# Seven block products for eight in the self-attention projections of a transformer block, with the context keys kept in device memory meanwhile

## The chip, the core and the metric

The kernel runs on one core of a Trainium2 chip. The core has a matrix engine (PE, with its weight loads shown as PEld), three engines for elementwise work (DVE, ACT and POOL) and an engine, SP, whose queue issues DMA transfers. Each engine takes its instructions in program order and waits on semaphores for the others. SBUF is the working memory of 128 partitions; PSUM, in eight banks of 512 fp32 values per partition, takes the matmul results. The metric is the device time of one execution in microseconds (us); a lower time is better.

## The reference

The reference is one transformer block in fp32 over x of shape (2, 1024, 256), with a context of shape (2, 154, 192): self-attention with 16 heads of 64, cross-attention to the context with as many heads, and a gated feed-forward.

```python
h = _layernorm(x, ln1_g, ln1_b)
x = _attention(h, h, sa_wq, sa_wk, sa_wv, sa_wo, sa_bo) + x
h = _layernorm(x, ln2_g, ln2_b)
x = _attention(h, cond_emb, ca_wq, ca_wk, ca_wv, ca_wo, ca_bo) + x
h = _layernorm(x, ln3_g, ln3_b)
p = h @ ff_w1 + ff_b1
a, gate = (p[..., :D_FF], p[..., D_FF:])
h = a * jax.nn.gelu(gate, approximate=False) @ ff_w2 + ff_b2
return h + x
```

Inside `_attention`, q = xq @ wq and k = xkv @ wk (256 or 192 channels by 1024 outputs), the scores are scaled by 1/8, go through a softmax and weigh v, and wo brings the result back to 256 channels. So the queries and keys of self-attention are two products of the same h with two weight matrices.

## The kernel before

The work on self-attention goes by units. A unit is one batch entry and one pair of heads, so there are 16 units, and a pair of heads has 128 columns of wq, of wk and of wv. The normalized tokens of a batch entry lie transposed in `hT`: 64 channels of one half of the tokens in the upper 64 partitions, the same 64 channels of the other half in the lower, and four blocks of channels side by side.

A unit has eight slots of 128 queries, p = 8 * unit + n with n from 0 to 7. The text below calls them slot 0 to slot 7. Every slot makes two groups of scores (`scores`, PE, L492; two PSUM banks for each group, two groups in all, so that a group can only be written once the exponents of the same group of the slot before have been read). DVE takes the maxima of each group (L501), ACT the exponents (L507: two instructions for each group, each with a read of its sum). The maxima and sums of the two halves of a row lie in different partitions, so four DMAs swap them (`exchange`, L517, on SP). POOL forms the differences (L525, L526), ACT their exponents (L532), POOL the denominators (L534, L536); this is done in the slot after. One slot later still, DVE takes the reciprocals (L604, between the two maxima), POOL scales the exponents with them (L612) and DVE transposes them (L639, two per slot). The transposed rows of four slots together are weighed with the values (`weigh`, PE, L546, one half in each of two slots).

The order of the instructions on each engine is the order in which the Python code emits them; no planner moves them. In the loop over p, `self_first` emits the scores and the maxima, `flush(stores)` emits copies out of PSUM that earlier pieces left, `then()` emits exponents, softmax steps, exchange and transposes, and after these comes a piece of PE work for the slot:

- slots 0, 3, 4 and 7: half of a `weigh`; the two copies of its result to SBUF (ACT, L678) come at the start of slots 1 and 5
- slot 1: the queries of the next unit (`self_queries`, L361, 64 matmul instructions of 512 columns)
- slot 2: the keys of the next unit (the same size)
- slot 5: the values of the next unit (L392), and one step of a norm running beside
- slot 6: two pieces of the output projection `py_sa` (L466), added to x by DVE (L473) one slot later each, and one step of a norm

The queries and keys go to two PSUM banks of the pool `mm`, and ACT copies them to SBUF at the start of the next slot (L376 with the scale, L384 with a regrouping of the keys); `weigh` and some other pieces use the two banks of the pool `po`. SP also issues the weights for the unit after next: wq in slot 2, wk in slot 3, wv in slot 7.

The context stage has 48 steps c, three for each unit (two of three tiles of tokens and one of two), with n = 0, 1, 2 within a unit. A step makes scores (L855), maxima (L860), exponents (L873) and, two steps later, transposes (L900). Eight DMAs regroup the transposed rows of a unit (`cross_regroup`, L917) into a buffer, `pairs`, that exists once; two steps later `cross_weigh` weighs the values with it (L938), with its first two results in the `po` banks and the other two in the `mm` banks, each copied by DVE (L955). For even units, `context_values` makes the values of two units (L813), ACT copies them (L823), and six DMAs complete them (L825, L830). The queries of the unit after next need a weight slice loaded by L133. Four output pieces of self-attention are left over at step 4; they run in steps 4 and 5. The context keys `kT` are computed during self-attention into an SBUF buffer of 320 columns for each of eight pairs. The gated feed-forward, which already uses seven products for eight, is last.

## Time and profile before

| | us |
|---|---|
| median of three runs | 1083.98 |
| lowest and highest of the three | 1083.78, 1085.25 |
| the profiled execution | 1085.11 |
| span of the profiled execution, first to last instruction | 1083.3 |
| PE busy in the span | 1067.4 |
| DVE busy | 889.9 |
| POOL busy | 765.0 |
| ACT busy | 646.9 |

The busy time of PE counts each matmul until its modelled end, and matmuls overlap, so a busy PE may still be issuing more slowly than it could; the distance between the starts of groups of matmuls says how fast it goes. A row of the timeline has its start in us from the start of the span, its length, engine, line, operation, the tiles written and read with their shapes, the number of merged instructions and, in brackets, how long the engine had been idle and what ended that. A row of the chain of work has start, length and what ran. A row of the waits has the waiting instruction, what it waited for, total us, times, and the longest. The clock granted to the matrix engine is 1.00 throughout.

### The profile page before, as it was taken

Reading aid. Unit: us, or ns where it says so; the run is one execution under the profiler, and the core shown is the slowest. Engines: PE = TensorE matmul, PEld = TensorE weight load, DVE = VectorE, ACT = ScalarE, POOL = GpSimd, SP = SyncE. Lnnn points to the kernel's source line nnn. Section 1 sums busy time; section 2 is a strip of 40 time slices with the busy share of each in tenths; the row PEclk is TensorE's granted clock in tenths of the full one; section 3 lists DMA queues with packets and bytes.
Section 4 is the critical chain, followed back from the end, with each engine's and each line's share of the span. In section 5 each row is a group of like instructions: output and inputs, shape, how many; then the busy total and the mean of one; then the engine's idle time right before and its main releaser. Section 6 shows DMA issues by size and latency. Waiting matters only on the chain.

```text
span 1083.3 us, 45246 instructions
## 1 busy us (share of the span) xinstructions
PE 1067.4 (99%) x18548; PEld 710.0 (66%) x18548; DVE 889.9 (82%) x1317; ACT 646.9 (60%) x2063; POOL 765.0 (71%) x1600
## 2 busy tenths in 40 slices
PE   8999999999999999999999999998999999999998
PEld 6556556566565565565675665575777767888998
DVE  5789999998998989999999989968877887655554
ACT  5666767677666666666776766666566554342221
POOL 2667777788777777777777777757665686388774
PEclk9999999999999999999999999999999999999999
DMA  3232111111111111211211201136855545000000
GB/s 94 64 90 62 44 43 44 37 38 43 33 43 24 43 43 33 48 42 29 48 41 26 53 14 37 24 96 139 202 134 138 126 115 131 17 6 15 20 11 30
DMA packets 105120, 62.84 MB, mean 58 GB/s; under 512 B 32266, under 2 KB 95506, under 8 KB 104914
## 3 DMA queue, kind: packets, MB, share of 16 engines
q1 hardware_dynamic: 103586, 59.29, 23.2%
q8 instruction: 146, 2.39, 0.9%
q10 hardware_dynamic: 1328, 0.66, 0.2%
q14 instruction: 60, 0.49, 0.1%
HBM read 30.01 MB, written 2.10 MB: 30 GB/s over the span
## 4 chain that ended last, share of the span: by engine, by line
PE 87%; DVE 3%; DMA 3%; POOL 3%; ACT 2%; SPq 1%; issue 1%; DVEq 0%; POOLq 0%; ACTq 0%
PE s L492 19%; PE po L546 19%; PE py_sa L466 5%; PE py_ca L466 5%; PE pv_sa L392 5%; PE pq_ca L361 4%; PE pq_sa L361 4%; PE pk_sa L361 4%; PE poc L938 4%; PE pb L1062 3%; PE pf L1186 3%; PE sc L855 3%; PE pa L1062 2%; PE pc L1062 2%; DMA st<-st 2%; PE pf L1225 1%
## 5 line engine op out<-in xcount | busy, mean ns | idle before, releaser
L612 POOL TENSOR_SCALAR p<-p,rd,ee 128x512 f32<-128x512 f32 x508 | 387.3, 773 | 99.1 <-DVE rd L604 97.3
L507 ACT ACTIVATE p<-s,st 128x512 f32<-128x512 f32 x512 | 345.8, 686 | 176.5 <-DVE st L501 170.5
L501 DVE TENSOR_REDUCE st<-s 128x2 f32<-128x1024 f32 x256 | 308.5, 1206 | 51.7 <-issue 20.1
L639 DVE STREAM_TRANSPOSE pT<-p 128x1024 f32<-128x1024 f32 x256 | 302.3, 1219 | 1.5 <-POOL p L612 1.5
L492 PE MATMUL s<-k_sa,q_sa 64*32 64x512 f32 x4096 | 255.4, 591 | 2.7 <-ACT p L507 2.1
L546 PE MATMUL po<-pT,v_sa 64*32 64x256 f32 x8192 | 238.6, 376 | 0.9 <-ACT p L873 0.9
L546 PEld LDWEIGHTS po<-pT,v_sa 64*32 64x32 f32 x8192 | 173.8, 106 | 74.9 <-issue 27.3
L492 PEld LDWEIGHTS s<-k_sa,q_sa 64*32 64x32 f32 x4096 | 81.6, 106 | 102.8 <-issue 53.5
L873 ACT ACTIVATE p<-sc,neg 128x154 f32<-128x154 f32 x256 | 96.5, 408 | 84.5 <-DVE rden L881 80.7
L884 POOL TENSOR_SCALAR p<-p,rden 128x154 f32<-128x154 f32 x256 | 97.3, 401 | 62.7 <-DVE rden L881 62.3
L507 ACT ACTIVATION_READ_ACCUMULATOR p<-s,st 128x1 f32 x512 | 103.2, 202 | 0.0
L525 POOL TENSOR_TENSOR dd<-st 128x8 f32<-128x8 f32 x128 | 25.8, 202 | 66.1 <-DMA st<-st 64.3
L392 PEld LDWEIGHTS pv_sa<-sa_wv,hT_ln 64*128 64x128 f32 x1024 | 58.6, 188 | 14.2 <-issue 10.9
L392 PE MATMUL pv_sa<-sa_wv,hT_ln 64*128 64x128 f32 x1024 | 61.8, 275 | 0.0
L860 DVE TENSOR_REDUCE neg<-sc 128x6 f32<-128x924 f32 (+1 forms) x48 | 48.0, 1001 | 14.5 <-PE sc L855 14.4
L466 PE MATMUL py_ca<-ca_wo,o_ca 128*128 128x256 f32 x256 | 59.9, 382 | 0.0
L466 PE MATMUL py_sa<-sa_wo,o_sa 128*128 128x256 f32 x256 | 59.5, 386 | 0.0
L466 PEld LDWEIGHTS py_sa<-sa_wo,o_sa 128*128 128x128 f32 x256 | 47.3, 190 | 17.8 <-issue 6.9
L361 PE MATMUL pq_ca<-hT_ln,ca_wq 64*128 64x512 f32 (+1 forms) x352 | 58.4, 590 | 0.5 <-DMA ca_wq<-in_L_xattn_ca_wq_dram 0.5
L873 ACT ACTIVATION_READ_ACCUMULATOR p<-sc,neg 128x1 f32 x256 | 57.2, 224 | 0.0
L361 PE MATMUL pq_sa<-hT_ln,sa_wq 64*32 64x512 f32 (+1 forms) x976 | 57.0, 586 | 0.0
L361 PE MATMUL pk_sa<-hT_ln,sa_wk 64*32 64x512 f32 x960 | 56.8, 590 | 0.0
(135 smaller groups left out, 1471.5 us busy)
## 6 DMA issues: line engine op xcount, KB each, us to landing
wf<-pT_ca SPq DMA_DIRECT2D x128, 128.0 KB, 2.4
v_sa<-v_sa SPq DMA_DIRECT2D x32, 256.0 KB, 3.8
st<-st SPq DMA_DIRECT2D x510, 1.0 KB, 1.9
sa_wq<-in_L_xattn_sa_wq_dram SPq DMA_DIRECT2D x32, 128.0 KB, 3.4
sa_wk<-in_L_xattn_sa_wk_dram SPq DMA_DIRECT2D x32, 128.0 KB, 3.6
sa_wv<-in_L_xattn_sa_wv_dram SPq DMA_DIRECT2D x32, 128.0 KB, 3.3
ca_wq<-in_L_xattn_ca_wq_dram SPq DMA_DIRECT2D x32, 128.0 KB, 4.4
wf<-in_L_xattn_ff_w_dram SPq DMA_DIRECT2D x12, 256.0 KB, 4.2
```

Of the source, the lines that this page charges most:

```text
L361: nc.tensor.matmul(pq[r][f:f + m, at:at + n], lhsT=wt[own, c, f:f + m], rhs=h[own, c, t0:t0 + n], start=(c == 0), stop=(c == NH - 1), tile ...
L392: nc.tensor.matmul(pv[r][:, i * P:(i + 1) * P], lhsT=h[own, c, i * P:(i + 1) * P], rhs=wt[own, c, :], start=(c == 0), stop=(c == NH - 1), ...
L466: nc.tensor.matmul(py[:, e * D:(e + 1) * D], lhsT=o[:, i, (t + e) * P:(t + e + 1) * P], rhs=wo[kind, b, g][:, i, :], start=(i == 0), stop= ...
L492: nc.tensor.matmul(sc[a4 * KB:(a4 + 1) * KB, j, :], lhsT=q[r, c:c + KB], rhs=k[r, h * HB:(h + 1) * HB], start=True, stop=True, tile_positi ...
L501: nc.vector.tensor_reduce(st[:, 0, 0, i, :], sc, AX.X, ALU.max, negate=True)
L507: nc.scalar.activation(pr[:, j, :], sc[:, j, :], AF.Exp, bias=st[:, 0, 0, i, j:j + 1], accum_out=st[:, 0, 1, i, j:j + 1],)
L546: nc.tensor.matmul(po[a2][d:d + KB, :QH // 2], lhsT=v[r, t, e, d:d + KB], rhs=pT[r, d // DH * NK + n, :], start=(t == 0 and e == 0), stop= ...
L612: nc.gpsimd.tensor_scalar(pr[:, j, :], pr[:, j, :], v["rd"][:, c:c + 1], v["ee"][:, 0, c:c + 1], op0=ALU.mult, op1=ALU.mult,)
L639: nc.vector.transpose(halves[h][:, :, c:c + KB], slot[p]["members"][i].rearrange("p j (n k) -> p (j n) k", k=KB))
L873: nc.scalar.activation(pr_[:, j, i, :T], sc[:, j, i * T:(i + 1) * T], AF.Exp, bias=neg[:, j, i:i + 1], accum_out=den[:, j, i:i + 1],)
L884: nc.gpsimd.tensor_scalar(pr_[:, j, i, :T], pr_[:, j, i, :T], rden[:, j, i:i + 1], 1.0, op0=ALU.mult, op1=ALU.mult,)
L1062: nc.tensor.matmul(into[:, :BT], lhsT=lhs, rhs=wh[pair][i], start=first, stop=True, skip_group_check=True)
```

## The change

Queries and keys of a unit are one product of a two by two block matrix (two halves of the tokens' blocks by two halves of the channels) with another (two halves of the channels by wq and wk). The new code forms this product with seven block products in place of eight. For each product, PE runs 16 matmuls of 256 columns (`product`, called 1 to 7). It applies to units 2 to 15; units 0 and 1 keep the old way.

- The sums of blocks are formed ahead by POOL: four of tokens for each batch entry (`held_tokens`, 128x512), and four of weights for each unit (`held_weights`, 128x256, mostly one each in slots 5, 6, 7 and 0). They lie in SBUF where `kT` was.
- In slot 1, behind the first two exponents, product 1 goes to one half of the two `mm` banks (`sums`), and ACT copies it to the queries. At the end of the slot products 2 and 5 go to the two halves of the `po` banks (`low`, `high`), product 6 adds to `sums`, and DVE joins `low` to the queries.
- At the start of slot 2, ACT copies `sums` and `high` out. Between the first and second exponents of slot 2, product 7 adds to `sums` and ACT copies the result to keys. At the end of the slot product 3 adds to `high`, product 4 to `sums`, DVE joins `high` to the queries, and POOL adds two halves of the keys (128x512). The last copy of keys, by ACT, follows in slot 3.
- The `mm` and `po` banks are no longer taken from pools, one tile a bank, but are two tiles of two banks each, of which `bank_of` hands out one bank and then the other.
- The context keys of pairs 0 to 5 are written to device memory when made, and come back by six DMAs in slots 4 to 7 of unit 14 and 0 and 1 of unit 15, when the sums are no longer needed; those of pairs 6 and 7 are made in place.
- In units 2 and 3, slot 6 takes two steps of the norm beside in place of one.
- In the context stage, the four left-over output pieces run one each in steps 4, 5, 7 and 10. In step 7 the values of unit 2 are made behind `cross_weigh` in place of before it. In units 4 and 5 the third step may also take a norm step that needs a bank.

```diff
--- before.py
+++ after.py
@@ -61,18 +61,24 @@
     small = ctx.enter_context(tc.tile_pool(name="small", bufs=4))
     pt_ = ctx.enter_context(tc.tile_pool(name="pt", bufs=2))
...
-    ps_m = ctx.enter_context(tc.tile_pool(name="ps_m", bufs=2, space=bass.MemoryType.PSUM))
-    ps_o = ctx.enter_context(tc.tile_pool(name="ps_o", bufs=2, space=bass.MemoryType.PSUM))
+    ps_2 = ctx.enter_context(tc.tile_pool(name="ps_2", bufs=1, space=bass.MemoryType.PSUM))
+    dram = ctx.enter_context(tc.tile_pool(name="dram", bufs=1, space=bass.MemoryType.DRAM))
     scored = ExitStack()
...
+    two = {what: ps_2.tile([P, 2, HB], F32, name=f"two_{what}") for what in ("mm", "po")}
+    turns = {"mm": 0, "po": 0}
+
+    def bank_of(what):
+
+        turns[what] ^= 1
+        return two[what][:, turns[what], :]
+
     def mm_tile(name):
-        return ps_m.tile([P, HB], F32, tag="mm", name=name)
+        return bank_of("mm")
 
     def sum_tile(name):
-
-        return ps_o.tile([P, HB], F32, tag="po", name=name)
-
+        return bank_of("po")
 
     xt = {
         (b, g): const.tile([P, GT, D], F32, tag=f"x{b}{g}", name=f"x{b}{g}")
...
     nc.gpsimd.memset(ctxT, 0.0)
-    kT = const.tile([P, NPAIR, B * TP], F32, tag="kT", name="kT")
+    keys = {"dram": dram.tile([P, NPAIR - 2, B * TP], F32, name="keys")}
+    held_sums = one.tile([P, NPAIR * B * TP], F32, tag="kT", name="sums")
+    last_sum = one.tile([P, 2, P], F32, tag="ws", name="last_sum")
+
+    def load_back(pr):
+
+        if pr == 0:
+            keys["sb"] = one.tile([P, NPAIR, B * TP], F32, tag="kT", name="kT")
+        nc.sync.dma_start(out=keys["sb"][:, pr, :], in_=keys["dram"][:, pr, :])
 
     def together(*pieces):
         dones = [piece() for piece in pieces]
...
+    HT = S // 4
+    tokens, seven = {}, {}
+
+    def held_tokens(b):
+
+        t = held_sums[:, :NH * S // 2].rearrange("p (k c t) -> p k c t", k=NH, c=NH // 2)
+        h = hT["sa", b]
+        h11, h12, h21, h22 = (
+            h[:, c:c + 2, j * HT:(j + 1) * HT] for c in (0, 2) for j in range(2))
+        tokens[b] = {
+            1: h11, 2: h21, 3: h22, 4: t[:, 2], 5: t[:, 0], 6: t[:, 1], 7: t[:, 3],
+        }
+        own = tokens[b]
+        sub = lambda x, y, z: lambda: nc.gpsimd.tensor_tensor(x, y, z, ALU.subtract)
+        return [
+            sub(own[5], h12, h11), sub(own[6], h22, own[5]), sub(own[4], h21, own[6]),
+            sub(own[7], h22, h12),
+        ]
+
+    def held_weights(pr):
+
+        t = held_sums[:, NH * S // 2:].rearrange("p (k c f) -> p k c f", k=2, c=2)
+        q, k = (wsl["sa", pr, what] for what in "qk")
+        seven[pr] = {
+            1: q[:, 0:2], 2: q[:, 2:4], 3: last_sum, 4: k[:, 2:4], 5: t[:, 0], 6: t[:, 1],
+            7: k[:, 0:2],
+        }
+        own = seven[pr]
+        tt = lambda x, y, z, op: lambda: nc.gpsimd.tensor_tensor(x, y, z, op)
+        return [
+            tt(own[5], own[7], own[4], ALU.add),
+            tt(own[6], own[5], own[1], ALU.subtract),
+            tt(own[7], own[1], own[7], ALU.subtract),
+            tt(own[3], own[2], own[6], ALU.subtract),
+        ]
+
+    def both_halves(x, j):
+        return x.rearrange("p (r u t) -> p u r t", r=2, u=2)[:, j]
+
+    def key_halves(x, j):
+        return x.rearrange("p (h r u n j) -> p u r n h j", h=2, r=2, u=2, j=KB)[:, j]
+
+    def projected(unit):
+
+        b, pr = unit
+        sums = two["mm"][:, :, :HT]
+        low, high = (two["po"][:, :, j * HT:(j + 1) * HT] for j in range(2))
+
+        def product(i, into, first):
+
+            wt, h = seven[pr][i], tokens[b][i]
+            for c in range(2):
+                for f in range(0, P, KB):
+                    for r in range(2):
+                        own = slice(r * HR, (r + 1) * HR)
+                        nc.tensor.matmul(
+                            into[f:f + KB, r, :], lhsT=wt[own, c, f:f + KB], rhs=h[own, c, :],
+                            start=(first and c == 0), stop=(c == 1),
+                            tile_position=(r * HR, f), skip_group_check=True,
+                        )
+
+        def queries(j):
+            return both_halves(qk["sa", b, pr][0], j)
+
+        def keys_of(j, src):
+
+            nc.scalar.copy(
+                key_halves(qk["sa", b, pr][1], j),
+                src.rearrange("p r (n h j) -> p r n h j", h=2, j=KB))
+
+        def start():
+            self_unit(b, pr)
+            product(1, sums, True)
+            nc.scalar.activation(queries(0), sums, AF.Copy, scale=scale)
+
+        def join(src, j):
+            nc.vector.scalar_tensor_tensor(
+                queries(j), src, scale, queries(j), op0=ALU.mult, op1=ALU.add)
+
+        def first():
+            product(2, low, True)
+            product(5, high, True)
+            product(6, sums, False)
+            join(low, 0)
+
+            def store():
+                nc.scalar.activation(queries(1), sums, AF.Copy, scale=scale)
+                keys_of(0, high)
+
+            stores.append(store)
+
+        def middle():
+            product(7, sums, False)
+            keys_of(1, sums)
+
+        def last():
+            product(3, high, False)
+            product(4, sums, False)
+            join(high, 1)
+            k = qk["sa", b, pr][1].rearrange("p (h r u t) -> p u h r t", h=2, r=2, u=2)
+            nc.gpsimd.tensor_tensor(k[:, 1], k[:, 1], k[:, 0], ALU.add)
+            kept.append(lambda: keys_of(0, sums))
+
+        return start, first, middle, last
...
-    def exponents(u, sc, st, i):
+    def exponents(u, sc, st, i, between=None):
 
         pr = pp_.tile([P, 2, HB], F32, tag="P", name=f"p_{u}")
         for j in range(2):
+            if j and between:
+                between()
             nc.scalar.activation(
                 pr[:, j, :], sc[:, j, :], AF.Exp, bias=st[:, 0, 0, i, j:j + 1],
                 accum_out=st[:, 0, 1, i, j:j + 1],
@@ -694,8 +815,10 @@
             reciprocals(p - 2)
         maxima(sc[1], st, 1)
 
-        def then():
-            members = [exponents(f"{p}_0", sc[0], st, 0)]
+        def then(between=None, behind=None):
+            members = [exponents(f"{p}_0", sc[0], st, 0, between)]
+            if behind:
+                behind()
             softmax_steps(p)
...
-            work.extend(nxt)
+            work.extend(nxt[2:] if ui else nxt)
...
-        return lambda: nc.scalar.copy(kT[:, pr, :], pk[:, :B * TP])
+
+        def store():
+            own = keys["sb" if "sb" in keys else "stage"][:, pr, :]
+            nc.scalar.copy(own, pk[:, :B * TP])
+            if "sb" not in keys:
+                nc.sync.dma_start(out=keys["dram"][:, pr, :], in_=own)
+
+        return store
...
-        q, k = qk["ca", b, pr], kT[:, pr, b * TP:b * TP + T]
+        q, k = qk["ca", b, pr], keys["sb"][:, pr, b * TP:b * TP + T]
...
-                other = kT.rearrange("p a b -> p (a b)")[:, :NF * BT].rearrange(
+                other = keys["sb"].rearrange("p a b -> p (a b)")[:, :NF * BT].rearrange(
                     "p (f t) -> p f t", f=NF)
...
+        keys["stage"] = p2.tile([P, NPAIR - 2, B * TP], F32, tag="hT", name="keys_stage")
         stats, deviation, normalize, turn = norm_pieces("sa", 0, True)
         spare["bank"] = sum_tile
...
+        parts_of, sums_due, due = {}, {}, {}
+        for i, slot_of in enumerate((3, 4, 5, 6)):
+            sums_due.setdefault(slot_of, []).append((held_tokens, 0, i))
+        for i, (u, n) in enumerate(((NPAIR - 2, 3), (NPAIR - 2, 4), (NPAIR - 2, 7), (NPAIR - 1, 0))):
+            sums_due.setdefault(u * 2 * SH + n, []).append((held_tokens, 1, i))
+        for ui in range(2, NU):
+            at = ((ui - 2) * 2 * SH + n for n in ((7, 7, 8, 8) if ui == 2 else (5, 6, 7, 8)))
+            if ui == NPAIR:
+                at = ((ui - 2) * 2 * SH + n for n in (5, 6, 8, 9))
+            for i, p in enumerate(at):
+                sums_due.setdefault(p, []).append((held_weights, units[ui][1], i))
         for p in range(SA):
             if p % (2 * SH) == 0:
                 self_beside(p // (2 * SH))
@@ -1308,19 +1450,35 @@
                 held.clear()
             then = self_first(p)
             flush(stores)
-            then()
+            ui, n = divmod(p, 2 * SH)
+            steps = None
+            if 0 < ui < NU - 1 and n in (1, 2):
+                steps = parts_of[ui + 1] = parts_of.get(ui + 1) or projected(units[ui + 1])
+            if steps and n == 1:
+                then(behind=steps[0])
+            elif steps:
+                then(between=steps[2])
+            else:
+                then()
             if adds:
                 adds.pop(0)()
             flush(kept)
-            ui, n = divmod(p, 2 * SH)
             if later and (p < 4 or n in (2, 4, 6) and p < SA - 2):
                 later.pop(0)()
             if p in ahead:
                 ahead[p]()
+            for fn, of, i in sums_due.get(p, ()):
+                if i == 0:
+                    due[fn] = fn(of)
+                due[fn][i]()
             load_ahead(p)
-            if p < 2 * SH - 1 or p % SH in (1, 2):
-
-                run_work(2 if p < SA - SH else 1, n > SH or p < SH, sum_tile)
+            if SA - SH - 8 <= p < SA - SH - 2:
+                load_back(p - SA + SH + 8)
+            if steps:
+                steps[1 if n == 1 else 3]()
+            elif p < 2 * SH - 1 or p % SH in (1, 2):
+
+                run_work(2 if p < SA - SH else 1, (1 + (ui in (2, 3) and n == SH + 2)) * (n > SH or p < SH), sum_tile)
                 if p == LAG:
                     load_weights("sa", units[1][1], "v")
                 if p == 3 * SH + 2:
@@ -1398,16 +1556,19 @@
                 run_work(0, 1, sum_tile if outs else None)
                 flush(stores)
                 run_work(0, 0, n_sum=1)
-                if ui % 2 == 0:
+                if ui % 2 == 0 and ui > 2:
                     run(lambda: context_values(*units[ui]))
-                run_work(1, 0)
+                if ui > HP + 1:
+                    run_work(1, 0)
                 flush(adds)
                 flush(stores)
                 cross_weigh(c)
+                if ui == 2:
+                    run(lambda: context_values(*units[ui]))
             elif n == 2:
-                run_work(0, 1, sum_tile if ui == HP + 1 else None)
+                run_work(0, 1, sum_tile if HP < ui < 3 * HP else None)
                 if c == SH + 1:
-                    run_work(2, 0)
+                    run_work(1, 0)
                 elif ui > HP and ui % HP == 1:
                     load_out("ca", *divmod(ui // HP - 1, NQ))
             cross_regroup(c)
```

## The prediction

> **What bounds the kernel now.** I read the page first, for the busy shares and the chain that ended last.
>
> ```profile
> span 1083.3 us, 45246 instructions
> PE 1067.4 (99%) x18548; PEld 710.0 (66%) x18548; DVE 889.9 (82%) x1317; ACT 646.9 (60%) x2063; POOL 765.0 (71%) x1600
> PE 87%; DVE 3%; DMA 3%; POOL 3%; ACT 2%; SPq 1%; issue 1%; DVEq 0%; POOLq 0%; ACTq 0%
> sa_wq<-in_L_xattn_sa_wq_dram SPq DMA_DIRECT2D x32, 128.0 KB, 3.4
> ```
>
> PE carries 87% of the chain. By this view, PE work taken away is time taken away. Whether that holds in the slots where the change works is seen in the timeline of one unit: slot 1 starts at 408.39, slot 2 at 413.54, slot 3 at 418.69.
>
> ```profile
> 405.14 3.45 PE po L546 x128
> ...
> 410.89 2.80 ACT p L507 x8
> ```
>
> ```profile
> 408.39 1.92 PE L492 MATMUL s<-k_sa,q_sa 64*32 64x512 f32 x32
> 409.07 0.65 DVE L473 TENSOR_TENSOR x<-py_sa,x 128x512 f32<-128x512 f32 x1
> 409.65 1.21 DVE L501 TENSOR_REDUCE st<-s 128x2 f32<-128x1024 f32 x1
> 410.11 3.64 PE L361 MATMUL pq_sa<-hT_ln,sa_wq 64*32 64x512 f32 x64
> 412.01 2.36 DVE L639 STREAM_TRANSPOSE pT<-p 128x1024 f32<-128x1024 f32 x2
> 413.54 1.92 PE L492 MATMUL s<-k_sa,q_sa 64*32 64x512 f32 x32
> 413.84 1.09 ACT L376 ACTIVATE q_sa<-pq_sa 128x512 f32<-128x512 f32 x2
> 414.77 1.22 DVE L501 TENSOR_REDUCE st<-s 128x2 f32<-128x1024 f32 x1 [0.40 <-ACT q_sa L376]
> 416.03 0.69 ACT L507 ACTIVATE p<-s,st 128x512 f32<-128x512 f32 x1 [1.10 <-DVE st L501]
> 417.11 2.36 DVE L639 STREAM_TRANSPOSE pT<-p 128x1024 f32<-128x1024 f32 x2
> 418.60 0.21 ACT L507 ACTIVATION_READ_ACCUMULATOR p<-s,st 128x1 f32 x1
> 418.69 1.92 PE L492 MATMUL s<-k_sa,q_sa 64*32 64x512 f32 x32
> ```
>
> The first fence is the chain of work (start, length, what), the second the timeline. A slot lasts 5.15: scores 1.72 (410.11 - 408.39), then a projection of 3.43 (413.54 - 410.11). PE issues without a gap. But DVE works from 414.77 to 419.47 in slot 2, 4.70 of 5.15, and ACT reads its last sum at 418.81, 5.27 after the slot's start. The slot's own chain (scores, maxima, exponents, next scores) is thus nearly as long as PE's work. An earlier slot that happens to have little PE work shows what that chain allows:
>
> ```profile
> 94.65 1.95 PE L492 MATMUL s<-k_sa,q_sa 64*32 64x512 f32 x32
> 99.73 0.21 ACT L507 ACTIVATION_READ_ACCUMULATOR p<-s,st 128x1 f32 x1
> 100.00 1.09 PE L492 MATMUL s<-k_sa,q_sa 64*32 64x512 f32 x16 [0.25 <-ACT p L507]
> ```
>
> The second group of the next slot starts 5.35 after this slot's start, 0.06 after ACT's last read, and PE waited for ACT. In a normal slot that group starts at 5.15 + 0.86 = 6.01 (0.86 is half of the scores' 1.72). So the reserve of a slot is 0.66, and no saving beyond it can arrive.
>
> The waits between 62 and 691 us say how often the reserve is touched:
>
> ```profile
> PE s L492 <- ACT p L507: 1.0, 4, 0.3
> ...
> DVE rd L604 <- POOL den L536: 10.5, 21, 1.5
> ```
>
> DVE waits 10.5 us for denominators, PE only 1.0 for the exponents behind them: the reserve now swallows nearly all of it.
>
> **The change part by part.** *Products.* `weigh` has 128 instructions of 256 columns in 3.45, 27 ns each. A product is 32 instructions, 0.86; seven are 6.04 where queries and keys take 2 x 3.43 = 6.86. PE saves 0.82 for each of 14 units, 11.5 us. Slot 1 becomes 1.72 + 4 x 0.86 = 5.17 and slot 2 1.72 + 3 x 0.86 = 4.31: the whole saving lies in slot 2.
>
> *What arrives of it.* In slot 2 a copy of keys now stands on ACT between the first two exponents; half of the 1.09 at 413.84 is 0.545. The chain of slot 2 becomes 5.35 + 0.545 = 5.90, against 6.01 now. PE will stand still for 5.90 - 4.31 - 0.86 = 0.73 before the second scores of slot 3 (or partly earlier, at product 4, which needs that copy too), and 0.11 of the 0.82 arrives: 14 x 0.11 = -1.5 us.
>
> *Product 6 in slot 1* overwrites what ACT copies to the queries behind two exponents. These start 2.50 after the slot's start (410.89) and four take 2.7 of the row's 2.80, so two end at 3.84, the copy at 4.39, and 0.05 later PE may go; it arrives at 1.72 + 3 x 0.86 = 4.31. That is 0.13 in each unit, bounds 0 and 0.3: +1.8 us.
>
> *Joins on DVE*, two in each unit. Their form (128x512, PSUM and SBUF in) has no row; the bounds are these, and I take 0.65, the row of equal width.
>
> ```profile
> L473 DVE TENSOR_TENSOR x<-py_sa,x 128x512 f32<-128x512 f32 x24 | 15.6, 652 | 0.0
> L1101 DVE SCALAR_TENSOR_TENSOR own<-pb,cols,own 128x256 f32<-128x256 f32 x14 | 6.8, 484 | 12.2 <-PE pb L1062 12.1
> L1153 POOL TENSOR_TENSOR wx<-wf,wx 128x512 f32<-128x512 f32 x2 | 2.5, 1274 | 0.0
> L319 POOL TENSOR_TENSOR x<-x,sa_bo 128x256 f32<-128x256 f32 x16 | 11.7, 731 | 0.0
> ```
>
> The lower bound is 0.48, the upper twice that. The add at 409.07 holds DVE 0.58 (to 409.65). DVE's slot of 4.70 becomes 5.28, longer than slot 1 (5.17) and than slot 2. Slot 1's transposes end at 414.37, its join at about 414.95, and slot 2's maxima could start at 414.77 + 0.13: no reserve is left. Any lateness of the denominators in slots 1 to 3 now reaches PE. That is 42 of about 120 slots, so 10.5 x 42 / 120 = 3.7 us exposed; some of it overlaps with waits counted above. I take +2.5 us, bounds 0 and 7.4 (twice 3.7, since exponents of slots 1 and 2 also end 0.55 later, and the exchange behind them).
>
> *POOL* gets four sums of 0.73 in slots 5, 6, 7 and 0, an addition of 1.27 in slot 2, and eight token sums of 1.27 in all. The sums of 0.73 stand where the bias additions of equal length stand today without PE waiting. The addition of 1.27 stands ahead of the scaling in slot 3, and with the later exponents of slot 2 it delays the denominators that slot 4 needs. +1.0 us, bounds 0 and 3.
>
> *Context keys.* Six writes and six reads of 160 KB (128 partitions x 320 x 4 B) join SP's queue, one in a slot, behind that slot's exchange; the nearest row is wq with 128 KB and 3.4 us. They are needed only later; they can delay a swap of maxima. +0.3 us, bounds 0 and 1.5. The new home of the PSUM banks, the FF's use of the returned tile, and the doubled norm steps (the same instructions, earlier) I set at nothing: PE has its full list of work in those slots.
>
> *Context stage.* Around steps 7 to 12, PE waits:
>
> ```profile
> 733.64 1.01 PE L855 MATMUL sc<-kT,q_ca 64*128 64x154 f32 x12
> 735.64 1.09 PE L938 MATMUL poc<-wf,v_ca 64*64 64x256 f32 x16
> 738.95 0.87 PE L938 MATMUL poc<-wf,v_ca 64*64 64x256 f32 x10 [1.36 <-ACT v_ca L823]
> 746.38 0.65 PE L938 MATMUL poc<-wf,v_ca 64*64 64x256 f32 x4 [0.19 <-DMA wf<-pT_ca]
> 750.32 0.86 PE L938 MATMUL poc<-wf,v_ca 64*64 64x256 f32 x10 [0.72 <-DMA wf<-pT_ca]
> 754.60 3.82 PE L361 MATMUL pq_ca<-hT_ln,ca_wq 64*128 64x512 f32 x15 [0.47 <-DMA ca_wq<-in_L_xattn_ca_wq_dram]
> 764.47 1.09 PE L938 MATMUL poc<-wf,v_ca 64*64 64x256 f32 x16
> 767.22 1.58 PE L855 MATMUL sc<-kT,q_ca 64*128 64x154 f32 x20
> ```
>
> ```profile
> 739.78 3.25 SPq L830 DMA_DIRECT2D v_ca<-ends  x4
> 743.13 5.27 SPq L917 DMA_DIRECT2D wf<-pT_ca  x8
> ```
>
> ```profile
> 737.56 0.18 DVE L240 BATCH_NORM_AGGREGATE mv_ln<-st_ln 128x2 f32<-128x6 f32 x1
> 740.39 1.58 PE L855 MATMUL sc<-kT,q_ca 64*128 64x154 f32 x20
> 751.76 0.79 PE L855 MATMUL sc<-kT,q_ca 64*128 64x154 f32 x8
> ```
>
> Undisturbed, `cross_weigh` takes 2.75 (764.47 to 767.22). In step 7 it takes 4.75 (735.64 to 740.39), in step 10 5.38 (746.38 to 751.76), and the queries of step 12 wait 0.47: 2.0 + 2.6 + 0.5 = 5.1 us. With the values behind `cross_weigh`, the DMAs of L825 and L830 fall behind the regrouping on SP's queue, which then starts some 5 us earlier, so the DMA waits of steps 10 and 12 go. But the output piece now put directly ahead of `cross_weigh` sits in one of the `po` banks that `cross_weigh` needs, and its add on DVE stands behind the step's reduction, transposes and statistics, which in step 7 end at 737.74, 4.1 after the step's start. Add 0.65: the bank comes free at 4.75, while PE is there at 0.95 + 1.85 (half of a 3.7 pair) + 0.4 = 3.2. That is 1.5 us in step 7, and about 1.8 in step 10, where no other piece covers it. In step 7 the values then wait 0.8 for DVE to empty an `mm` bank. So step 7 goes from 2.0 to 2.3 or 2.6 (+0.5), step 10 from 2.6 to 1.8 (-0.8), step 12 gains 0.5 to 0.8. I take -1.0 us, bounds -4.5 (all waits gone but 0.6) and +1.
>
> The sum: -1.5 + 1.8 + 2.5 + 1.0 + 0.3 - 1.0 = +3.1 us. Against the profiled execution's 1085.11 that is 1088.2; the median of the runs is 1.13 below it, so 1087.1.
>
> **The rivals.** *Faster: the context stage's waits go and little comes back in self-attention.* Place: steps 7 to 12. If DVE does the pieces' adds before PE needs the bank, -4.5 stands in place of -1.0; with half of the joins' term (+1.2) and of POOL's (+0.5) the sum is -2.2 us, 1081.8, and down to 1078 with those terms at zero. It decides where DVE has less than 2.3 us of work queued ahead of the add. For it: DVE idles between steps in this stage. Against it: the step's own work stands first.
>
> *Faster by much: the chain of slot 2 does not bind,* 11.5 us arrive, about 1071.5 with the context's -1.0. The wait at 100.00 speaks against it.
>
> *No change:* the denominators mostly come in time, joins and POOL cost 0.5 together, the rest as above: -1.5 + 1.8 + 0.5 + 0.3 - 1.0 = +0.1, 1084.1.
>
> *Slower by more: the two halves of a bank are not independent.* Slot 3's `weigh` writes the left halves of the `po` banks, the second join reads the right halves. If it must wait for the join, its reserve shrinks: the join ends 1.36 + 4.70 + 0.58 = 6.64 after slot 2's start (1.36 being the later maxima), `weigh` starts at 5.90 + 0.86 = 6.76. Then DVE's lateness hits PE twice, the joins' term is at its 7.4, POOL's at 2: sum +9.0, 1093. [...] No run so far shows it.
>
> **How the numbers follow.** Differences under 0.2% (2.2 us) can hardly be told from no change with this kernel. Forecast case (slower by 1 to 6 us) 0.45; slower by more 0.12; no change 0.18; faster 0.22; faster by much 0.03. A part of the forecast case lies within 0.2%: slower 0.48, same 0.27, faster 0.25. The range reaches from the faster rival's lower end to the slower rival: 1078 to 1093; the forecast's own is 1084.5 to 1090.
>
> **What would show it.** Right: in slot 3 the second scores wait some 0.7 for ACT's exponents (or product 4 for a key copy), slots 1 to 3 together are no shorter than now (15.5), PE's waits for ACT in self-attention grow from 1.0 to about 10 us, DVE is over 95% busy in slots 1 and 2. In the context stage `cross_weigh` waits for DVE's add where it waited for DMA. Wrong: slot 2 lasts 4.3 with no wait behind it; or products take more than 0.86; or units grow by a microsecond in slots 4 to 7, through POOL.

## The result and the profile after

The changed kernel takes 1147.88 us (median of four executions, 1147.41 to 1150.27), the kernel before 1084.1: 1.0586 times as long, 95% interval 1.0573 to 1.06. The profiled execution took 1150.27 us, its span is 1148.3. It lies 55 us above the upper end of my range. The page after, first the line of busy times, then the slices of the span for PE and its clock, then the chain that ended last:

```profile
PE 1087.0 (95%) x19892; PEld 730.6 (64%) x19892; DVE 906.3 (79%) x1345; ACT 653.5 (57%) x2077; POOL 826.2 (72%) x1678
...
PE   8999889999999999999999999987899889899997
...
PEclk9999989999999999999999999998999889999999
...
PE 53%; DVE 13%; POOL 10%; DMA 7%; ACT 6%; issue 5%; SPq 4%; DVEq 0%; POOLq 0%; ACTq 0%
```

PE is busy for 95% instead of 99%, and the chain runs through PE for 53% of the span instead of 87%. The slices name the places: the fifth and sixth (115 to 172 us), and from the 27th on (746 us) the context stage and the start of the feed-forward. The waits of PE, longest in total first:

```profile
PE two_po L585 <- DVE hT_ln L304: 17.3, 5, 4.8
PE two_po L293 <- ACT xn_ln L283: 6.5, 3, 5.8
PE two_mm L1192 <- DVE x L592: 4.5, 5, 1.4
PE two_po L1068 <- DVE x L592: 2.9, 3, 1.8
PE two_po L667 <- ACT hT_ln L308: 2.5, 1, 2.5
...
PE two_mm L520 <- ACT q_sa L538: 1.9, 5, 0.6
PE two_mm L520 <- ACT k_sa L531: 1.5, 3, 0.7
...
PE s L611 <- ACT p L628: 1.4, 5, 0.6
```

The waits of which my prediction spoke (products L520, scores L611) stand further down. The first belongs to no part that I had costed: an output piece (L585), whose result goes to one of the two `po` banks, waits five times for DVE to empty the other one. Here is the longest of the five in the timeline after, in step 13 of the context stage:

```profile
780.93 0.66 PE L293 MATMUL two_po<-ident,xn_ln 128*128 128x128 f32 x4 [0.57 <-POOL xn_ln L280]
784.99 1.35 DVE L304 TENSOR_SCALAR hT_ln<-two_po,cols 128x128 f32<-128x128 f32 x4
786.40 3.78 PE L585 MATMUL two_po<-ca_wo,o_ca 128*128 128x256 f32 x8 [4.82 <-DVE hT_ln L304]
```

and step 13 in the timeline before, with the same transposes, output piece and copies, where each bank is a tile of its own:

```profile
759.56 0.66 PE L279 MATMUL ph_ln<-ident,xn_ln 128*128 128x128 f32 x4
760.05 1.89 PE L466 MATMUL py_ca<-ca_wo,o_ca 128*128 128x256 f32 x8
761.85 1.36 DVE L290 TENSOR_SCALAR hT_ln<-ph_ln,cols 128x128 f32<-128x128 f32 x4
```

Before, DVE also came late to these copies, 1.80 us after the output piece had begun, and nobody waited. After, the piece waits 4.82, and then its eight matmuls take 3.78 instead of 1.89, twice the time: from 783.8 to 790.6 the clock granted to PE is at half (0.50). The second wait of the list stands in unit 2, slot 6. The timeline there, and below it the windows (stretch, length, busy time with instructions for PE, PEld, DVE, ACT and POOL, granted clock, DMA share, GB/s):

```profile
146.21 1.09 ACT L283 ACTIVATE xn_ln<-x,off_ln,rstd_ln 128x256 f32<-128x256 f32 x2 [1.22 <-DVE off_ln L269]
147.35 1.11 PE L293 MATMUL two_po<-ident,xn_ln 128*128 128x128 f32 x4 [5.80 <-ACT xn_ln L283]
148.26 5.65 PE L585 MATMUL two_mm<-sa_wo,o_sa 128*128 128x256 f32 x16
```

```profile
145.00:152.00 7.00, 4.65 (x13) 3.93 (x14) 1.66 (x6) 2.60 (x6) 3.13 (x7) 0.54 0.20 45
152.00:165.00 13.00, 13.00 (x344) 8.10 (x351) 9.92 (x12) 6.30 (x20) 7.20 (x15) 0.99 0.07 17
```

Two norm steps stand in this slot. The second, the transposes of L293, needs the tokens that the first has normalized only after DVE and ACT have been through their own queues, and PE, which takes its list in order, stands for 5.80 with two output pieces behind.

And the part that I had worked out, slots 1 to 3, in the timeline after (the slots of unit 9, in which the queries and keys of unit 10 are made; the 16 matmul calls of a product are 32 instructions in the trace, and the product groups are written to `two_mm` and `two_po`):

```profile
428.90 1.92 PE L611 MATMUL s<-k_sa,q_sa 64*32 64x512 f32 x32
432.79 0.59 ACT L538 ACTIVATE q_sa<-two_mm 128x512 f32<-128x512 f32 x1
433.53 1.10 PE L520 MATMUL two_mm<-sums 64*32 64x256 f32 x32
434.39 1.95 PE L611 MATMUL s<-k_sa,q_sa 64*32 64x512 f32 x32
434.76 0.65 DVE L541 SCALAR_TENSOR_TENSOR q_sa<-two_po,q_sa 128x512 f32<-128x512 f32 x1
437.56 0.57 ACT L531 COPY k_sa<-two_mm 128x512 f32<-128x512 f32 x1
438.19 1.10 PE L520 MATMUL two_mm<-sums,sa_wk 64*32 64x256 f32 x32
439.08 2.22 PE L611 MATMUL s<-k_sa,q_sa 64*32 64x512 f32 x32
441.09 3.66 PE L667 MATMUL two_po<-pT,v_sa 64*32 64x256 f32 x128
444.54 1.93 PE L611 MATMUL s<-k_sa,q_sa 64*32 64x512 f32 x32
```

The slots last 5.49, 4.69 and 5.46, 15.64 together, where they took 15.47. PE issues 0.82 less, but product 6 starts at 433.53 behind the copy of the queries, product 4 at 438.19 behind the copy of the keys, and slot 3's scores take 2.01 to the start of `weigh` where 1.72 is their own time: nothing of the 0.82 arrives. Unit 9 is an undisturbed one. Over all 14 units in whose slots products are made (1 to 14), the three slots are 6.3 us longer than before, 0.45 a unit, because some have a longer slot 1 (6.01 in unit 10).

Where the 65.0 us of the two profiled spans came from is seen by the start of each stage, taken from the first matmul of its scores or gate products (us; for the experiments, told of below, what the stage starts later than in the kernel before):

| start of | before | after | banks_alone | one_step | own_banks | own_banks_one_step |
|---|---|---|---|---|---|---|
| unit 2 | 104.33 | +2.5 | +1.0 | +2.5 | +2.4 | +2.3 |
| unit 4 | 189.88 | +17.7 | +2.3 | +3.8 | +16.6 | +5.4 |
| context stage | 701.62 | +21.3 | +1.3 | +12.8 | +24.6 | +15.3 |
| feed-forward | 910.74 | +54.3 | +29.9 | +50.4 | +26.8 | +18.2 |
| end | 1083.31 | +65.0 | +40.7 | +61.0 | +26.6 | +18.1 |

Units 2 and 3 cost 15.2 us, units 4 to 15 3.6 in all, and from the context stage on, where none of the new products is left, come 43.7. The experiments of the table ran on another chip, where the kernel before has a span about 1.3 us longer, so that much at the end of their columns is the chip.

### The profile page after: what moved, and what is told of

Read it like the earlier page. It is cut to its first block, busy times and chain, and to the rows that moved or that the text cites. A ratio compares the mean times of both kernels' runs of the same rounds, so it can differ in the third digit from the quotient of the medians.

```text
span 1148.3 us, 48114 instructions
## 1 busy us (share of the span) xinstructions
PE 1087.0 (95%) x19892; PEld 730.6 (64%) x19892; DVE 906.3 (79%) x1345; ACT 653.5 (57%) x2077; POOL 826.2 (72%) x1678
## 4 chain that ended last, share of the span: by engine, by line
PE 53%; DVE 13%; POOL 10%; DMA 7%; ACT 6%; issue 5%; SPq 4%; DVEq 0%; POOLq 0%; ACTq 0%
PE two_po L667 9%; PE s L611 8%; DMA st<-st 6%; POOL p L733 6%; PE two_mm L585 5%; DVE st L620 4%; SPq L638 4%; ACT p L628 4%; PE two_mm L375 4%; PE pb L1192 3%; PE two_mm L406 3%; PE two_po L1316 3%; PE two_po L585 3%; PE sc L985 3%; DVE pT L760 2%
## 5 line engine op out<-in xcount | busy, mean ns | idle before, releaser
L611 PE MATMUL s<-k_sa,q_sa 64*32 64x512 f32 x4096 | 255.7, 592 | 3.7 <-ACT p L628 1.4
L667 PE MATMUL two_po<-pT,v_sa 64*32 64x256 f32 x8192 | 238.5, 378 | 4.8 <-ACT hT_ln L308 2.5
L667 PEld LDWEIGHTS two_po<-pT,v_sa 64*32 64x32 f32 x8192 | 169.5, 107 | 85.3 <-issue 24.9
L611 PEld LDWEIGHTS s<-k_sa,q_sa 64*32 64x32 f32 x4096 | 75.3, 106 | 102.5 <-ACT p L628 40.5
L406 PEld LDWEIGHTS two_mm<-sa_wv,hT_ln 64*128 64x128 f32 x1024 | 58.5, 188 | 14.2 <-issue 10.9
L406 PE MATMUL two_mm<-sa_wv,hT_ln 64*128 64x128 f32 x1024 | 61.7, 275 | 0.0
L375 PE MATMUL two_mm<-hT_ln,ca_wq 64*128 64x512 f32 (+1 forms) x352 | 57.8, 590 | 0.0
L585 PE MATMUL two_mm<-sa_wo,o_sa 128*128 128x256 f32 x232 | 56.0, 396 | 0.9 <-ACT v_sa L415 0.9
L585 PEld LDWEIGHTS two_mm<-sa_wo,o_sa 128*128 128x128 f32 x232 | 44.4, 197 | 17.3 <-ACT v_sa L415 6.3
L1030 DVE STREAM_TRANSPOSE pT_ca<-p 128x480 f32<-128x480 f32 (+1 forms) x96 | 52.7, 585 | 0.7 <-POOL p L1014 0.5
L1229 ACT ACTIVATE own<-two_mm,cols 128x256 f32<-128x256 f32 x32 | 15.1, 473 | 65.8 <-PE two_mm L1192 65.8
L592 DVE TENSOR_TENSOR x<-two_mm,x 128x512 f32<-128x512 f32 x48 | 31.8, 666 | 23.6 <-PE two_mm L585 21.3
```

The source lines that it names most:

```text
L375: nc.tensor.matmul(pq[r][f:f + m, at:at + n], lhsT=wt[own, c, f:f + m], rhs=h[own, c, t0:t0 + n], start=(c == 0), stop=(c == NH - 1), tile ...
L406: nc.tensor.matmul(pv[r][:, i * P:(i + 1) * P], lhsT=h[own, c, i * P:(i + 1) * P], rhs=wt[own, c, :], start=(c == 0), stop=(c == NH - 1), ...
L585: nc.tensor.matmul(py[:, e * D:(e + 1) * D], lhsT=o[:, i, (t + e) * P:(t + e + 1) * P], rhs=wo[kind, b, g][:, i, :], start=(i == 0), stop= ...
L611: nc.tensor.matmul(sc[a4 * KB:(a4 + 1) * KB, j, :], lhsT=q[r, c:c + KB], rhs=k[r, h * HB:(h + 1) * HB], start=True, stop=True, tile_positi ...
L667: nc.tensor.matmul(po[a2][d:d + KB, :QH // 2], lhsT=v[r, t, e, d:d + KB], rhs=pT[r, d // DH * NK + n, :], start=(t == 0 and e == 0), stop= ...
L1030: nc.vector.transpose(pTc["ring"][:, ui % 3, :, j, t0 * KB:(t0 + nt) * KB].rearrange("p n (i q) -> p i n q", q=KB), pr_[:, j, :nt, :].rear ...
```

## The experiments

The theory after this reading: two banks in one tile hold up whoever writes the one until the other has been read (A), and two norm steps in a slot put PE behind a wait inside its own list (B); the products themselves cost little. The rival was that the products, through DVE and POOL, disturb everything behind them. (The expectations, written before each run, call the second theory C, and by rival B they mean the new order of the context stage.) The first four kernels ran on one chip (before: 1086.4 there).

**banks_alone.** The kernel before with nothing changed but the home of the banks:

```diff
+    two = {what: ps_2.tile([P, 2, HB], F32, name=f"two_{what}") for what in ("mm", "po")}
...
-        return ps_m.tile([P, HB], F32, tag="mm", name=name)
+        return bank_of("mm")
...
-        return ps_o.tile([P, HB], F32, tag="po", name=name)
+        return bank_of("po")
```

> The kernel before, with the mm and po banks as two tiles of two banks each and nothing else changed. Theory A (a write to one bank of such a tile also waits for reads of the other bank): the waits of output pieces for the norm's copy (L585 for L304 in the changed kernel, 17.3 us) and of the gate's products for adds appear here too, with half-clock stretches behind them: 1105 to 1127 us. Rival B (the new order of the context stage makes these waits, not the tiles): no change, 1082 to 1086 us.

It took 1125.77 us, 39 more than the kernel before, with eight products and one norm step as ever. Its waits:

```profile
PE two_po L472 <- DVE hT_ln L296: 18.1, 6, 4.6
PE two_mm L1068 <- DVE x L479: 4.5, 5, 1.4
```

They are the first and the third of the changed kernel, and self-attention, where all output pieces go to the `mm` banks and nearly all of a norm's transposes to the `po` banks, is only 1.3 us longer. A is shown, and it needs nothing else of the change. It is the program that asks for the wait, by its semaphores: in the kernel before, the same piece was written without it.

**one_step.** The changed kernel with one norm step in each slot; the token sums of the second batch entry move with them, to where its norm now ends:

```diff
-... run_work(..., (1 + (ui in (2, 3) and n == SH + 2)) * (n > SH or p < SH), sum_tile)
+... run_work(..., n > SH or p < SH, sum_tile)
...
-... ((NPAIR - 2, 3), (NPAIR - 2, 4), (NPAIR - 2, 7), (NPAIR - 1, 0)) ...
+... ((NPAIR - 2, 6), (NPAIR - 2, 7), (NPAIR - 1, 0), (NPAIR - 1, 1)) ...
```

> The changed kernel with one norm step in slot 6 in all units, and the token sums of the second batch entry moved to slots 6 and 7 of unit 6 and 0 and 1 of unit 7. Theory C (the second norm step in the slot makes PE wait for a whole norm, 5.8 us at 147.35 and 3.0 at 202.38, and the clock falls behind it): self-attention ends some 16 to 18 us earlier, 1128 to 1133 us. Rival (the waits belong to the coupled banks): 1144 us or more.

1146.33 us, far above what I expected. Its longest wait in total is that of the changed kernel:

```profile
PE two_po L585 <- DVE hT_ln L304: 17.4, 5, 4.8
```

The table shows that the edit did its work: the 5.80 wait is gone, and unit 4 starts 13.8 us earlier than in the changed kernel. Of this 5.3 are lost again in units 4 to 15, 1.8 of them in unit 7, where a product waits 1.5 for the token sums that now come later, so that the context stage starts 8.5 earlier. But from there to the end this kernel loses 48.3 where the changed one loses 43.7: the same five waits for the coupled bank stand in its context stage, and the clock is at half in six stretches there and in the feed-forward, 30.7 us together, in place of five with 23.9; that is 3.4 of the 4.6. The expectation forgot that what the coupled banks cost depends on when each wait falls.

**own_banks.** The changed kernel with a tile for each bank. A copy or join that covered two banks becomes two, one for each:

```diff
-    two = {what: ps_2.tile([P, 2, HB], F32, name=f"two_{what}") for what in ("mm", "po")}
+    two = {what: [ps_2.tile([P, HB], F32, name=f"{what}{r}") for r in range(2)] for what in ("mm", "po")}
...
-            nc.vector.scalar_tensor_tensor(
-                queries(j), src, scale, queries(j), op0=ALU.mult, op1=ALU.add)
+            for r in range(2):
+                nc.vector.scalar_tensor_tensor(
+                    queries(j)[:, r], src[r], scale, queries(j)[:, r], op0=ALU.mult, op1=ALU.add)
```

> The changed kernel with a tile for each of the four banks; copies and joins over two banks become two instructions each (5 copies and 2 joins a unit are 10 and 4). Theory A: the context stage and the feed-forward lose their waits, 30 to 43 us less than the changed kernel, 1105 to 1118 us; self-attention may lose a few us to the extra instructions. Rival B: 1146 to 1152 us.

1111.93 us, 25.5 over the kernel before on this chip, where the changed kernel is 63.8 over its own: 38 are gone, and from the context stage to the end the kernel loses only 2.0. Its waits begin with B, which is untouched:

```profile
PE po L293 <- ACT xn_ln L283: 6.3, 2, 5.7
PE s L615 <- ACT p L632: 3.1, 9, 1.0
PE po L671 <- ACT hT_ln L308: 2.7, 1, 2.7
```

**own_banks_one_step** (and, the same kernel on two other chips, both_mended and mended_again). Both mendings together.

> Both: a tile for each bank and one norm step a slot. If A and C are all there is beside the sum of the prediction, this gives that sum, 1087 us, with up to 3 us for the extra instructions: 1084 to 1092 us. A third cause would leave it above 1095 us.

> The mended kernel (a tile for each bank, one norm step a slot) once more, as the neighbour of the next run: 13 to 18 us over the kernel before on the same chip.

1102.1 us (1098.99 to 1103.44), 1.013 times the kernel before (1.0112 to 1.0149); 1098.93 and 1094.97 in one execution each on the other chips, where the kernel before took 1085.23 and 1084.21. So A and B were the greater part, about 39 and 9 to 10 us, and 11 to 16 remain, more than I expected. Most of them lie in self-attention: in mended_again 9.2 of the 9.7 us by which its span is longer. An undisturbed unit has 5.28, 4.72 and 5.67 in slots 1 to 3, 0.20 more than before, 2.8 for 14 units. But slots 1 to 3 of the 14 units are 9.4 longer in mended_again. The other 6.6 are single places, and what makes each of them late was not isolated; the largest is a wait in unit 7 for the token sums of the second batch entry, which this kernel makes later, since its norm steps come one in a slot:

```profile
PE mm L520 <- POOL sums L478: 1.7, 1, 1.7
```

**spread_alone.** The kernel before with the edits of the context stage alone (pieces spread over steps 4, 5, 7 and 10, values of unit 2 behind `cross_weigh`, a norm step in more third steps).

```diff
-                if ui % 2 == 0:
+                if ui % 2 == 0 and ui > 2:
                     run(lambda: context_values(*units[ui]))
-                run_work(1, 0)
+                if ui > HP + 1:
+                    run_work(1, 0)
...
                 cross_weigh(c)
+                if ui == 2:
+                    run(lambda: context_values(*units[ui]))
...
-                run_work(0, 1, sum_tile if ui == HP + 1 else None)
+                run_work(0, 1, sum_tile if HP < ui < 3 * HP else None)
                 if c == SH + 1:
-                    run_work(2, 0)
+                    run_work(1, 0)
```

> The kernel before with the context stage's edits alone: the left-over output pieces one each in steps 4, 5, 7 and 10, the values of unit 2 behind the weighing, norm steps with a bank in units 4 and 5 too. The prediction's own term: 1 us faster, at most 4.5 faster or 1 slower. Rival B (the new order costs the tens of us): 1100 us or more.

1085.78 us, 1.0002 times the kernel before (0.9993 to 1.0011): no change.

**values_behind.** Of these edits only the values of unit 2 behind `cross_weigh`.

> The kernel before with one edit: in step 7 the values of unit 2 are made behind the weighing. The waits of 2.0 us in step 7 and 2.6 in step 10 shrink, since the regrouping no longer queues behind the DMAs of the values, and the output pieces stay where they were, so no add stands before the bank: 2 to 4 us faster. If PE instead waits for a bank and for DVE as long as it waited for DMA: no change.

1083.14 us against 1085.23 on the same chip, ratio 0.9977 (0.9968 to 0.9986). This is the only kernel of the study that is faster than the kernel before. The waits of PE from 700 to 860 us, first of spread_alone, then of values_behind:

```profile
PE poc L938 <- DVE x L473: 1.9, 3, 1.2
PE po L546 <- ACT kT L780: 1.0, 1, 1.0
```

```profile
PE pv_ca L813 <- DVE o_ca L955: 1.4, 1, 1.4
PE poc L938 <- ACT q_ca L376: 0.9, 1, 0.9
```

With the values behind, the waits for the regrouping DMAs are gone in both. In values_behind the 2.4 us gained between steps 6 and 15 are kept. In spread_alone `cross_weigh` waits 1.2 us in step 7 and 0.2 in step 10 for the adds of the spread pieces on DVE, as the prediction had it; the gain of 2.05 that is left at the start of step 12 goes in steps 13 to 17, where the norm's transposes come later (0.68 each in steps 14 and 17) and PE waits 1.5 in step 13 for POOL and DVE. Which of this run's three edits makes the waits of step 13 was not separated.

**two_products_less.** The mended kernel with products 3 and 4 left out:

```diff
         def last():
-            product(3, high, False)
-            product(4, sums, False)
             join(high, 1)
```

> The mended kernel with products 3 and 4 left out (a part of queries and keys isn't computed): 1.72 us less of PE work in slot 2 of 14 units, 24 us in all. If the chain of scores, maxima, exponents and key copy sets slot 2, as the prediction has it, this time cannot be taken: within 4 us of the neighbour. If PE's work sets it: 20 to 24 us less.

It was 1106.2 us, 7 longer than its neighbour both_mended, and so outside the 4 us that I had allowed, with 24 us of PE work taken out (14 units, two products of 0.86). Its waits, and the timeline of one slot 3:

```profile
PE s L613 <- ACT p L630: 29.6, 29, 2.2
```

```profile
293.14 1.28 PE L520 MATMUL mm<-sums,sa_wk 64*32 64x256 f32 x32
296.15 1.09 PE L613 MATMUL s<-k_sa,q_sa 64*32 64x512 f32 x16 [1.73 <-ACT p L630]
297.49 1.96 PE L613 MATMUL s<-k_sa,q_sa 64*32 64x512 f32 x16 [0.24 <-ACT p L630]
```

The work that PE no longer does comes back as 29.6 us of waiting for the exponents: slots 1 to 3 of an undisturbed unit stay at 15.67, to the hundredth. The chain through maxima, exponents and copy, and not PE, sets the time here. And in six units idle times of 1.7 to 2.2 us put the clock to half (0.50 from 605 to 608, behind the one of 1.97 that ended at 603.53), so that 16 matmuls took 1.96 in place of 1.09: 10 us longer in the slots 3 of these units together, more than the whole 7.

**joins_small, copy_behind, neither** (one chip, with mended_again as neighbour at 1094.97): which of the two, the joins on DVE or the copy of keys between the exponents, ate the saving.

```diff
# joins_small
-                    queries(j)[:, r], src[r], scale, queries(j)[:, r], op0=ALU.mult, op1=ALU.add)
+                    queries(j)[:, r, :1], src[r][:, :1], scale, queries(j)[:, r, :1], op0=ALU.mult, op1=ALU.add)
# copy_behind
             product(7, sums, False)
-            keys_of(1, sums)
...
             product(4, sums, False)
+            keys_of(1, high)
```

> The mended kernel (a tile for each bank, one norm step per slot) as the neighbour of the three that follow. Near 1099 to 1102 us; undisturbed units have 5.28, 4.72 and 5.67 us in slots 1, 2 and 3, 15.67 together.

> The mended kernel with each join on DVE cut from 256 columns a bank to one (so most queries lack four of the seven products; the output is not the reference's). If the copy of keys between the exponents is what eats the saving, slots 1 to 3 lose only what the join delays the maxima by, 0.1 to 0.2 us a unit: 15.5, and the time falls by 1 to 4 us. If the joins are the price, as my term of +2.5 us (up to 7.4) had it, the time falls by 5 to 8 us.

> The mended kernel with the copy of half of the keys taken out from between slot 2's exponents and put behind them, from the other bank's halves (so one block of the keys takes products 3 and 5 in place of 7; the output is not the reference's). If that copy eats the saving, product 4 no longer waits for it (slot 2 falls from 4.72 to about 4.31) and the second scores of slot 3 come 5.34 instead of 5.99 after slot 2's start (slots 2 and 3 together from 10.39 to about 9.65): 0.74 in 14 units, the time falls by 8 to 11 us. If something else holds slots 2 and 3 (PE's own work, the joins), it falls by less than 3.

> Both of these edits together (queries and keys incomplete). If copy and joins together are the whole of what ate the saving, slots 1 to 3 come to about 14.7 (5.17, 4.31, 5.22), 0.97 below the mended kernel's, and the time falls by 11 to 14 us, to within 2 us of the kernel before or under it. If the unit stays above 15.3, something that neither edit touches holds it.

1096.13, 1098.0 and 1096.81 us: neither alone nor both together gave anything. (mended_again itself came out below its 1099 to 1102, with the slots as expected.) Slots 1 to 3 say why:

| undisturbed unit | slot 1 | slot 2 | slot 3 | sum |
|---|---|---|---|---|
| mended_again | 5.28 | 4.72 | 5.67 | 15.67 |
| joins_small | 5.28 | 4.72 | 5.67 | 15.67 |
| copy_behind, best | 5.28 | 4.31 | 5.73 | 15.32 |
| copy_behind, often | 5.28 | 4.31 | 6.05 | 15.64 |
| neither, best | 5.28 | 4.31 | 5.54 | 15.13 |

With the copy out of the way, product 4 does not wait and slot 2 falls by 0.41, as expected; but slot 3 grows. The timeline of copy_behind there, and its longest wait:

```profile
599.70 0.65 ACT L532 COPY k_sa<-po 128x256 f32<-128x256 f32 x2
600.24 0.71 DVE L544 SCALAR_TENSOR_TENSOR q_sa<-po,q_sa 128x256 f32<-128x256 f32 x2
...
601.01 3.69 PE L671 MATMUL po<-pT,v_sa 64*32 64x256 f32 x128
```

```profile
PE po L671 <- DVE q_sa L544: 5.3, 9, 1.3
```

`weigh` writes the left halves of the `po` banks and waits for the join that reads the right halves; the join stands behind DVE's transposes and, four times in this kernel, waits for the copy that I had moved, since both read the same halves. So the theory that the copy alone ate the saving fell, and so did that of the joins alone. The reading that fits is two strands of nearly equal length, one over ACT (exponents and copy), one over DVE (transposes and join), of which the longer one sets the slot. It is not shown strictly, since copy_behind brings a wait of its own, that of the join for the moved copy. With both out the best unit is 0.54 shorter, not the expected 0.97, and other units, 15.2 to 16.6, took it back. What would be the next strand was not followed further.

## Why the prediction was wrong

**The step that failed** is the sentence "The new home of the PSUM banks, the FF's use of the returned tile, and the doubled norm steps (the same instructions, earlier) I set at nothing: PE has its full list of work in those slots." The home of the banks measured 39 us alone (banks_alone), 38 taken back (own_banks); the doubled norm steps 8.5 to 9.3 by the start of the context stage (one_step against the changed kernel, own_banks_one_step against own_banks), of which 3.9 remained in the whole time with coupled banks, and 9.8 with a tile for each. The reason given was wrong for both: PE's list was full, but PE takes it in order, and these edits put a wait at its head. The diff showed it: `bank_of` returns a slice of one tile, and the trace before showed that a norm's copies on DVE run late (761.85) while the next output piece is already under way (760.05). I read that the buffers kept their number and size, and did not ask which instructions a shared tile would order.

With this step mended the sum of +3.1 would still have been too low: the mended kernel is 11 to 16 us over the kernel before. The parts show where.

**Products.** I had 0.11 of 0.82 arriving, and with product 6's wait and the joins a net loss of 0.20 a unit, 2.8 us in all. In the changed kernel slots 1 to 3 of an undisturbed unit lost 0.17 to 0.18, but of all 14 units 6.3 us (9.4 in mended_again): the forecast fits the undisturbed units, and the units that run late were mis-sized. The mechanism was right (scores of slot 3 behind the exponents, product 4 behind the copy of keys, both foreseen); two_products_less shows it: less PE work brings nothing. Of the signs that I had named, the slots no shorter than 15.5 came, and DVE busy for all of slot 1 and 96% of slot 2 of unit 9; PE's waits for ACT in self-attention did not grow to 10 us as a sum of idle time (2.6 for products and scores), the delay shows in the starts of the groups. Product 6's wait was mis-sized: 0.33 (433.53 against 433.20), taken as 0.13, bounds 0 and 0.3. The copy began at 3.89 and took 0.59, so that it ended 0.09 later than taken; PE followed 0.15 behind it, not 0.05.

**Joins.** Their price of 0.65 each is as taken (434.76). The term of +2.5 is not theirs: cut to one column (joins_small) they change nothing in an undisturbed unit as long as the copy is there, and slots 1 to 3 of the 14 units fall by 1.1 us of 9.4. The lateness that the term stood for is there, as the longer slots of single units, but not by the joins alone. What I called DVE's reserve looks like a second strand, not a sum.

**POOL and context keys** (+1.0 and +0.3). Slots 4 to 7 of units 4 to 14 are together no longer than before. The late sums cost 1.7 us once in the mended kernels and 0.2 in the changed one. In all kernels with the keys in device memory the first three steps of the context stage are 1.2 to 3.3 us longer, where I had 0.3 with a bound of 1.5, behind a swap of maxima that lands late; whether the returning keys delay it was not isolated.

**Context stage** (-1.0). Steps 3 to 11 became 1.05 us shorter in the changed kernel, 1.98 with a tile for each bank and 2.05 in spread_alone; the wait for DVE's add that I had named is in that sum (1.2 in step 7, taken as 1.5, and 0.2 in step 10, taken as 1.8). What I had not costed is what the later norm steps give back behind step 12. The rival of waits that go without a return is refuted for the edits together, and holds for one of them (values_behind) at half its size, 2.4 of 4.5. The lower end of this rival, 1078, was added up wrongly: with the joins and POOL at zero its terms give -3.9, 1080.

**The rival "slower by more".** Its premise, that `weigh` waits for a join in the other half of its bank, had no run behind it when it was written. Such waits are seen since: 5.3 us in copy_behind (nine, the longest 1.3), 0.2 in the changed kernel (one). Whether the bank or the tile that both halves share makes the program wait here, no run separates. It was not what decided: the coupling that cost 39 us is between two banks of one tile.

## What to carry to other kernels

When buffers change their home, list for each writer which readers the new tile puts ahead of it, and look in the trace for readers that are late today without harm; they are the price. An edit set at nothing because "PE has work" needs the order of that work: a wait at the head of a list hides behind nothing (5.80 us in unit 2, slot 6). And before counting on a saving in an engine at 99%, take some of its work out and see whether the slot gets shorter; there may be one or two strands of the same length beside it.

## What the runs showed of the hardware

A short wait of PE cost more than itself. In the kernel before, PE is never idle for over 1.4 us once started, and the granted clock is 1.00; in the changed kernel it is 0.985, and 1.5% of 1148.3 us is up to 17 of the 65. These are the idle times of PE over 1.6 us in the changed kernel once PE has started, and the stretches in which the clock was at half (0.50):

| PE idle, us | ended at | clock at half |
|---|---|---|
| 5.80 | 147.35 | 145.53 to 152.35 |
| 2.45 | 202.38 | 203.56 to 206.97 |
| 2.13 | 734.64 | not |
| 1.80 | 758.31 | not |
| 4.82 | 786.40 | 783.82 to 790.65 |
| 2.91 | 806.34 | 807.71 to 811.13 |
| 4.56 | 904.46 | 903.29 to 910.11 |
| 2.52 | 923.92 | 923.77 to 927.18 |
| 2.52 | 940.82 | 940.83 to 944.25 |

The three idle times of 4.56 to 5.80 came with 6.8 us at half clock each, the four of 2.45 to 2.91 with 3.4 each, and those of 1.80 and 2.13 with none. In two_products_less 1.73 with 0.24 behind it was enough (the rows at 296.15 and 297.49), and a wait of 2.99 did nothing. Three stretches of that kernel, as windows (the second number behind the stretch is PE's busy time):

```profile
294.12:297.53 3.41, 1.44 (x38) 0.23 (x26) 3.41 (x4) 3.41 (x11) 3.11 (x6) 1.00 0.02 3
727.57:730.98 3.41, 1.84 (x14) 0.76 (x10) 2.59 (x5) 3.41 (x14) 3.01 (x8) 1.00 0.30 89
730.98:734.40 3.42, 2.00 (x77) 1.78 (x85) 3.16 (x6) 3.42 (x17) 2.45 (x8) 1.00 0.02 5
```

In the first, PE is idle for 1.97, the waits of 1.73 and 0.24 shown above together, and the 16 matmuls that start at 297.49 take 1.96 in place of 1.09. The wait of 2.99 lies across the other two, 1.57 and 1.42 of it, and the clock stayed at 1.00 in both. So in these runs the length of a single wait does not tell whether it costs the clock: 1.73 with 0.24 behind it did, 2.13 and 2.99 did not. What else decides was not isolated.
